# Layer 1 of a conv-attention kernel: the last turns of four blocks by VectorE and DMA, one more half diagonal, and ACT issuing half of the moves

## The chip, the cores and the metric

The kernel runs on one core of a Trainium2 chip. The metric is device time in microseconds (us) of the whole launch. Engines are named as the profile names them: PE (TensorE), DVE (VectorE), ACT (ScalarE), POOL (GpSimd) and SP (SyncE, which here only issues DMAs). ACT issues DMAs too, in order with its own computing.

## What is computed

The reference, cut to what matters (x is 4 images of 128 channels and 4096 positions, float32):

```python
x = x + L0_conv(_gn(x))             # layer 0: attention over the positions, keys of width 64
t = _to_tokens(x)                   # 4 x 4096 tokens of 128
# layer 1, attention: queries and keys are the same matrix q
q = einsum('bsd,de->bse', _ln_t(t), W)
attn = softmax(einsum('bsd,btd->bst', q, q), axis=-1)
t = t + einsum('bst,btd->bsd', attn, _ln_t(t))
# layer 1, recurrence over blocks of the tokens
Wx = einsum('bti,hi->bth', _ln_t(t), W_ffn)    # normalised over the batch
y_t = sigmoid(Wx_t + y_{t-1} @ V.T)            # t = t + y
```

The scores of layer 1 are symmetric: score(s, t) = score(t, s). The kernel uses this.

## The kernel before

**Stages.** One image after the other goes through layer 0 (`layer0`) and layer 1 (`layer1`); after the fourth comes the recurrence (lines 910 to 990). Work on the next image (`prepare`: normalising, queries, keys, values, gates) lies in a list `ahead`, and the closing work of each block in a list `pending`. One entry of one of these is taken per step of the main loops. An empty entry (`nothing`) lets one entry of `ahead` pass. The program is then ordered engine by engine by the tile framework's scheduler, so that an engine's order differs in places from the order of the text[...].

**Layer 1, the pairs.** Tokens form 8 blocks of 512. The loop at line 775 takes n = 6, 7, 5, 4, 3, 2, 1, 0 and, inside, a = n down to 0. A pair (n, a) has two steps (i = 0, 1). In each, PE makes the scores of 512 queries of block n against two tiles of 128 keys of block a (L795, into `ps`, two buffers), ACT turns them into e = exp(score - 48) (L801, four buffers of e), and two steps later (`LAG`) PE adds the direct products h.T @ e to the block's sum `o` (L672, in `direct`). The token matrix h has had 1 added to it, so that the sum over the channels of a result gives the softmax denominator.

For a < n, DVE also turns e in 32x32 blocks into `dd` (L642, two buffers), and 16 DMAs put the blocks into place in `tt` (`send`, L652, three buffers): a quarter f of the rows of `tt` for each of four parts p. Before the change SP issues f = 0, 1, 2 at the end of the pair, and ACT issues f = 3 after the exp of the next step (`unsent`, line 807). Four steps after the pair's end PE multiplies the turned e with the tokens of block n (`reversed_products`, L685), which gives block n's share in block a. `part` (L694, L696) adds up the shares in `oacc`. The tiles `o` and `ot` share three PSUM buffers (`ps_o`).

**The diagonal, a = n.** For n > 1 (`upper`) only the half on and above the diagonal is computed, in columns 512, 384, 256 and 128 wide. Its 6 tiles off the diagonal are turned by DVE (L636), sent (L652, 12 smaller DMAs by SP and 4 by ACT), and multiplied by `own_products` (L662) three steps after the pair, behind that step's direct products. For n < 2 a different way is used: the first step is full, and in the second (`quarter`) PE computes two half-width scores (L581) and makes the rest by four PE transposes of the e before (L587), which ACT copies (L595).

**The end of a block.** When all shares are in, `finish` loads the residual tokens `t` (L722) and queues `tokens`, three empty places, `turn` and `inputs`. `tokens` turns `oacc` by four PE transposes into a PSUM tile (L727, `ps_m`, one buffer), takes the denominators, adds the residual and normalises into h2. `turn` turns h2 by four more PE transposes (L747), ACT copies them into `th` (L748), and the new tokens go out to `t2_d` by `turn_out` (DVE transpose L275, four DMAs L279). `inputs` multiplies `th` with the recurrence's weights (L756). Blocks 7, 6, 5 and 4 are complete in the first half of layer 1, since the pairs that give to them are taken first; blocks 3 to 0 close after pairs of their own.

`move` (used three times per block in layer 0) turns 32x32 blocks by DVE (L275), writes them to DRAM in four DMAs (L279, `turn_d`) and reads them back in place by one (L289): a full turn without PE.

Of the kernel before, what the change touches and what calls it, by code (L numbers as in the profile page):

```python
# [10 lines left out]
F32 = mybir.dt.float32  # L11
# [7 lines left out]
P = 128  # L19
# [153 lines left out]
def fast(  # L173
# [13 lines left out]
    with ExitStack() as st:  # L187
# [124 lines left out]
        def flat(t):  # L312
            return t.rearrange("q p j i -> q (p j i)")
# [237 lines left out]
        def layer1(b, h, qt):  # L551
# [7 lines left out]
            fifo: deque = deque()  # L559
            own_turned: deque = deque()  # L560

            unsent: deque = deque()
            turned: deque = deque()
            clock = 0
# [39 lines left out]

            def upper(n, a):

                return a == n > 1

# [45 lines left out]
            def own_products():  # L656

                _, n, t, o = own_turned.popleft()
                assert fifo and fifo[-1][0] == n
                t = t[:, : 4 * 6 * 32].rearrange("q (p s k) -> q p s k", p=4, s=6)  # L660
                for j, s in ((3, 3), (2, 1), (1, 0)):
                    nc.tensor.matmul(  # L662
                        o[:, : j * P], lhsT=h[:, NQ * n + j, :],
                        rhs=t[:, :, s : s + j, :].rearrange("q p k j -> q k p j"),
                        start=False, stop=False,
                    )
# [25 lines left out]
            def part(n, o):  # L692
# [7 lines left out]
                if parts[n] == NB - n - (b == B - 1 and n == 0):  # L700
                    finish(n)

            def finish(n):
                cs = bass.ts(n, QB)
                rinv = stat.tile([P, NQ], F32, tag="rinv", name="rinv")
                t = work.tile([P, 4, NQ, 32], F32, tag="t", name="t1", bufs=2)
                if b == B - 1 and n == 0:

                    one, two = (ep.tile([P, 2, QB], F32, tag="e", name="last") for _ in range(2))
                    h2, t1 = (one[:, r, :].rearrange("q (j c) -> q j c", j=NQ) for r in range(2))  # L710
                    th = two[:, 0, :]

                    def bank():
                        return ps_s.tile([P, 2, QB], F32, tag="s", name="ml")[:, 0, :]
                else:
                    h2 = work.tile([P, NQ, C], F32, tag="h2", name="h2")
                    th = work.tile([P, QB], F32, tag="th", name="th")
                    t1 = work.tile([P, NQ, C], F32, tag="og", name="t1b")

                    def bank():  # L720
                        return ps_m.tile([P, QB], F32, tag="m", name="m1")
                nc.sync.dma_start(t, t_d[b, n])  # L722

                def tokens():
                    m = bank().rearrange("q (j c) -> q j c", j=NQ)
                    for j in range(NQ):
                        nc.tensor.transpose(m[:, j, :], oacc[:, n, bass.ts(j, P)], ident)  # L727
                    at = (B + b) * NT + n * NQ
                    den = den_all[:, at : at + NQ]
                    nc.vector.tensor_reduce(den, m, AX.X, ALU.add)  # L730
                    nc.vector.tensor_scalar(den, den, 1.0 / C, None, ALU.mult)
                    nc.vector.reciprocal(rinv, den)
                    for j in range(NQ):
                        nc.vector.scalar_tensor_tensor(
                            t1[:, j, :].rearrange("q (p i) -> q p i", p=4),
                            m[:, j, :].rearrange("q (p i) -> q p i", p=4), rinv[:, j : j + 1],
                            t[:, :, j, :], ALU.mult, ALU.add,
                        )
                    layernorm(quarters(t1), quarters(h2))

                def result():
                    turn_out(t1.rearrange("q j (p i) -> q j p i", p=4), t2_d[b, :, cs])

                def turn():
                    m = bank()
                    for j in range(NQ):
                        nc.tensor.transpose(m[:, bass.ts(j, P)], h2[:, j, :], ident)  # L747
                    nc.scalar.copy(  # L748
                        th.rearrange("c (p j k) -> c j p k", j=NQ, p=4),
                        m.rearrange("c (j p k) -> c j p k", j=NQ, p=4),  # L750
                    )
                    result()

                def inputs():
                    m = bank()
                    nc.tensor.matmul(m, lhsT=wt["f"], rhs=th, start=True, stop=True)  # L756
                    nc.vector.bn_stats(bn_st[:, b * NB + n, :], m)
                    m = m.rearrange("p (g i s) -> p i g s", i=L // 2, s=2)
                    if b == B - 1:
                        nc.vector.tensor_copy(wxs[:, :, b, bass.ts(n, GB), :], m)  # L760
                    else:
                        wx = work.tile([P, L // 2, GB, 2], F32, tag="wx", name="wx")
                        nc.vector.tensor_copy(wx, m)
                        nc.sync.dma_start(wxs_d[b, :, :, bass.ts(n, GB), :], wx)

                if b == B - 1 and n == 0:
                    pending.appendleft(tokens)
                    pending.extend([turn, inputs])
                elif b == B - 1 and n < 4:
                    pending.extend([tokens, turn, inputs])  # L770
                else:
                    pending.extend([tokens, nothing, nothing, nothing, turn, inputs])


            for n in [NB - 2, NB - 1] + list(range(NB - 3, -1, -1)):
# [4 lines left out]
                for a in order(n):  # L780
# [4 lines left out]
                    for i in range(2):  # L785
                        ps = ps_s.tile([P, 2, QB], F32, tag="s", name="ps")
                        e = ep.tile([P, 2, QB], F32, tag="e", name="e")
                        if a == n < 2 and i == 1:
                            quarter(n, ps, e, before)
                        else:  # L790
                            width = 0
                            for half in range(2):
                                at = NQ * a + 2 * i + half
                                cols, scores = columns(n, a, i, half, ps)
                                nc.tensor.matmul(  # L795
                                    scores, lhsT=qt[:, bass.ts(at, P)],
                                    rhs=qt[:, n * QB + cols.start : n * QB + cols.stop],
                                    start=True, stop=True,
                                )
                                width += cols.stop - cols.start  # L800
                            nc.scalar.activation(  # L801
                                e.rearrange("p a b -> p (a b)")[:, :width],
                                ps.rearrange("p a b -> p (a b)")[:, :width], AF.Exp, bias=shift,
                            )
                            if turns(n, a) or upper(n, a):
                                turn_tiles(n, a, i, e, packed(d, n, a))
                        if unsent:
                            unsent.popleft()()
                        before = e
                        if o is None:  # L810
                            o = ps_o.tile([P, QB], F32, tag="o", name="o")
                        if n == NB - 2 and i == 0 and a > 0:
                            queries(a - 1)
                        elif n == NB - 2 and a == 0 and i == 1:
                            flush((b, NB - 1))
                            queries(NB - 1)
                        fifo.append((n, a, i, e, o))
                        clock += 1
                        if len(fifo) > LAG:
                            direct()  # L820
                            if a == order(n)[0] and i == 0:
                                direct()
                        if own_turned and own_turned[0][0] <= clock:
                            own_products()
                        if turned and turned[0][0] <= clock:
                            reversed_products()
                        if pending:
                            pending.popleft()()
                        elif ahead:
                            ahead.popleft()()  # L830
                    if turns(n, a) or upper(n, a):
                        send(n, a, d, t, nc.sync, range(3))
                        unsent.append(partial(send, n, a, d, t, nc.scalar, (3,)))
                    if upper(n, a):
                        own_turned.append((clock + 3, n, t, o))
                    elif turns(n, a):
# [555 lines left out]
```

## Time and profile before

| | us |
|---|---|
| runs | 3024.1, 3025.35, 3025.53 (median 3025.35) |
| profiled execution, device time | 3023.71 |
| its span | 3021.6 |
| layer 0, each image (stages 12 to 384, 776 to 1106, 1499 to 1829, 2221 to 2550) | 372, 330, 330, 329 |
| layer 1, each image (384 to 776, 1106 to 1499, 1829 to 2221, 2550 to 2930) | 392, 393, 392, 380 |
| recurrence and end | 91.6 |

How to read the profile's lines: a group line gives line, engine and operation, output<-input, shapes, the count, then busy time and the mean duration in ns, then the engine's idle time just before, with what ended it. A wait line reads "engine, output, line <- what it waited for: total us, times, longest". In lines in order of time the first number is the start from the span's begin, the second the length of the piece. PEld is PE's loading of weights, which runs beside the products. A name ending in q (SPq, ACTq) is the engine's DMA issue. The clock granted to PE was 0.992 of full speed.

### The profile page before, as it was taken

To read this page: it belongs to the slowest core of one execution; us is meant where nothing else is said; L and a number is where in the kernel's file an instruction comes from. 1 tells how busy PE (TensorE), PEld (TensorE's weight loads), DVE (VectorE), ACT (ScalarE), POOL (GpSimd) and SP (SyncE) were. 2 spreads that over 40 slices of the span, in tenths; PEclk is the share of its full clock that TensorE was granted. 3 is DMA by queue.
4 is the path that set the end of the run, shared out by engine and by line. 5 is a ranking of instruction groups with operands and counts; after the bars stand their busy time and mean duration, and the time that the engine had idled before them with its cause. 6 is when DMAs were issued, how large, how long until landed. Compare 5 with 4: busy or idle time off the path is not lost.

```text
span 3021.6 us, 32547 instructions
## 1 busy us (share of the span) xinstructions
PE 2963.2 (98%) x10768; PEld 1381.4 (46%) x10768; DVE 1718.1 (57%) x3210; ACT 1017.0 (34%) x1127; POOL 217.5 (7%) x215
## 2 busy tenths in 40 slices
PE   9999999999999999999999999999999999999985
PEld 4444444444444444444444444444444444444442
DVE  6666654544666664544466666454456666244446
ACT  3444422222344432232244443222234444222224
POOL 0011100000011100000011101000001101000000
PEclk9999999999999999999999999999999999999998
DMA  1111144334112124444311114443411113444433
GB/s 42 41 55 56 46 135 105 97 98 110 28 56 57 50 90 107 106 99 106 72 46 56 51 44 130 104 103 95 106 42 56 50 42 111 129 109 107 103 124 150
DMA packets 265425, 250.62 MB, mean 83 GB/s; under 512 B 96160, under 2 KB 180640, under 8 KB 264224
## 3 DMA queue, kind: packets, MB, share of 16 engines
q1 hardware_dynamic: 239328, 216.95, 26.6%
q10 hardware_dynamic: 25920, 31.49, 4.1%
q8 instruction: 89, 1.46, 0.2%
q14 instruction: 88, 0.72, 0.1%
HBM read 65.80 MB, written 56.62 MB: 41 GB/s over the span
## 4 chain that ended last, share of the span: by engine, by line
PE 94%; DVE 2%; DMA 2%; ACT 1%; SPq 1%; issue 0%; POOL 0%; DVEq 0%; ACTq 0%; POOLq 0%
PE o L476 29%; PE o L672 15%; PE ps L238 15%; PE ps L795 14%; PE ot L685 13%; PE o L662 1%; PE m L756 1%; PE m L267 1%; PE mp L369 1%; PE mp L438 1%; DMA tt<-dd 1%; DMA wxs<-wxs_d 1%; PE mp L423 1%; DVE t2s L976 1%; DVE ps_r L949 1%; SPq L652 1%
## 5 line engine op out<-in xcount | busy, mean ns | idle before, releaser
L476 PE MATMUL o<-e,nxt 64*128 64x512 f32 x4096 | 966.5, 589 | 0.0
L240 ACT ACTIVATE e<-ps 128x1024 f32<-128x1024 f32 x512 | 520.9, 1023 | 688.3 <-PE ps L238 648.8
L247 DVE TENSOR_TENSOR acc<-acc,e 128x1024 f32<-128x1024 f32 x448 | 548.5, 1224 | 229.3 <-ACT e L240 212.7
L476 PEld LDWEIGHTS o<-e,nxt 64*128 64x128 f32 x4096 | 400.5, 187 | 482.6 <-issue 473.8
L801 ACT ACTIVATE e<-ps,shift 128x1024 f32<-128x1024 f32 (+2 forms) x282 | 298.4, 1059 | 730.4 <-PE ps L795 417.0
L238 PE MATMUL ps<-nxt 64*128 64x512 f32 x2048 | 533.3, 595 | 1.2 <-ACT e L240 0.6
L672 PE MATMUL o<-e,h 128*128 128x512 f32 (+3 forms) x1160 | 511.0, 567 | 0.0
L795 PE MATMUL ps<-qt 128*128 128x512 f32 (+3 forms) x1128 | 502.0, 567 | 4.0 <-ACT qt L574 2.7
L642 DVE STREAM_TRANSPOSE dd<-e 128x512 f32<-128x512 f32 x444 | 287.4, 687 | 309.7 <-ACT e L801 215.8
L685 PE MATMUL ot<-tt,h 128*128 128x512 f32 x888 | 402.3, 593 | 0.0
L672 PEld LDWEIGHTS o<-e,h 128*128 128x128 f32 x1160 | 220.3, 191 | 258.5 <-issue 247.9
L795 PEld LDWEIGHTS ps<-qt 128*128 128x128 f32 x1128 | 208.3, 190 | 229.8 <-issue 207.9
L238 PEld LDWEIGHTS ps<-nxt 64*128 64x128 f32 x2048 | 195.1, 187 | 229.4 <-issue 148.8
L685 PEld LDWEIGHTS ot<-tt,h 128*128 128x128 f32 x888 | 164.4, 190 | 186.7 <-issue 185.6
L145 POOL TENSOR_SCALAR rstd<-mv 128x4 f32<-128x4 f32 x64 | 14.5, 226 | 2355.9 <-DVE mv L300 2355.9
L694 DVE TENSOR_TENSOR oacc<-oacc,ot 128x512 f32<-128x512 f32 x87 | 59.4, 682 | 161.8 <-PE ot L685 161.8
L532 DVE SCALAR_TENSOR_TENSOR t<-yt,rinv,t 128x128 f32<-128x128 f32 x128 | 36.5, 347 | 82.4 <-DMA yt<-turn_d 82.4
L543 POOL TENSOR_SCALAR h<-h 128x512 f32<-128x512 f32 x32 | 72.4, 2261 | 63.8 <-DVE d L275 61.7
L493 POOL TENSOR_SCALAR xb<-xb,bpc 128x512 f32<-128x512 f32 x32 | 58.1, 1815 | 245.5 <-DMA xb<-in_x_dram 230.2
L146 POOL TENSOR_TENSOR rstd<-rstd,mhalf 128x4 f32<-128x4 f32 x64 | 66.4, 1037 | 5.3
L381 ACT ACTIVATE nxt<-mp,par 64x512 f32<-64x512 f32 x31 | 23.9, 772 | 115.7 <-DVE nxt L377 99.8
L303 DVE TENSOR_SCALAR h<-t,mv,rstd 128x128 f32<-128x128 f32 x128 | 35.7, 343 | 46.8 <-POOL rstd L146 46.8
(159 smaller groups left out, 1583.8 us busy)
## 6 DMA issues: line engine op xcount, KB each, us to landing
tt<-dd SPq DMA_DIRECT2D x1332, 64.0 KB, 2.0
tt<-dd ACTq DMA_DIRECT2D x444, 64.0 KB, 2.0
turn_d<-d SPq DMA_DIRECT2D x384, 64.0 KB, 1.8
nxt<-in_x_dram SPq DMA_DIRECT2D x16, 512.0 KB, 5.5
xb<-in_x_dram SPq DMA_DIRECT2D x32, 256.0 KB, 3.3
t<-turn_d SPq DMA_DIRECT2D x32, 256.0 KB, 2.7
yt<-turn_d SPq DMA_DIRECT2D x32, 256.0 KB, 2.6
t_d<-t SPq DMA_DIRECT2D x32, 256.0 KB, 2.0
```

Source lines behind the costliest of these rows:

```text
L146: nc.gpsimd.tensor_tensor(dst, dst, mhalf[:, :n], ALU.pow)
L238: nc.tensor.matmul(ps[:, h, :], lhsT=lhsT, rhs=rhs, start=True, stop=True)
L240: nc.scalar.activation(e, ps, AF.Exp, scale=scale)
L247: nc.vector.tensor_tensor(acc, acc, e, ALU.add)
L476: nc.tensor.matmul(o[r], lhsT=v[rs, p + h * PAIRS, :], rhs=e[rs, h, :], start=(p == 0 and h == 0), stop=(p == PAIRS - 1 and h == 1),)
L543: nc.gpsimd.tensor_scalar(hn, hn, 1.0, None, ALU.add)
L642: nc.vector.transpose(d.rearrange("q f b k j -> q k b f j")[:, 2 * i + half], e[:, half, :].rearrange("q (b f j) -> q b f j", b=NQ, f=NQ),)
L672: nc.tensor.matmul(o[:, cols], lhsT=h[:, NQ * a + 2 * i + half, :], rhs=es, start=(a == order(n)[0] and i == 0 and half == 0), stop=(a == ...
L685: nc.tensor.matmul(ot, lhsT=h[:, NQ * n + j, :], rhs=t.rearrange("q (p b k j) -> q b k p j", p=4, b=NQ, k=NQ)[:, j], start=(j == 0), stop= ...
L694: nc.vector.tensor_tensor(oacc[:, n, :], oacc[:, n, :], o, ALU.add)
L795: nc.tensor.matmul(scores, lhsT=qt[:, bass.ts(at, P)], rhs=qt[:, n * QB + cols.start : n * QB + cols.stop], start=True, stop=True,)
L801: nc.scalar.activation(e.rearrange("p a b -> p (a b)")[:, :width], ps.rearrange("p a b -> p (a b)")[:, :width], AF.Exp, bias=shift,)
```

## The change

1. `upper` holds for n > 0: block 1's diagonal is computed as a half as well, and `quarter` remains for n = 0 alone.
2. `own_products` is taken ahead of the step's direct products. (Its check that the newest entry belongs to block n becomes one that some entry does.)
3. Of a turned pair's moves, SP issues f = 0, 1 and ACT f = 2 and f = 3, one each after the exps of the next two steps. A diagonal's moves stay 12 and 4.
4. For n >= 4 `finish` calls `finish_moved`. It turns `oacc` by `move` into `otk` in place of the PE transposes, and after three empty places takes denominators, residual and normalisation from `otk`, with the sum written over `t`; h2 goes by a second `move` into `th` in place of the PE transposes and ACT's copy, the new tokens go out as before, and after three more empty places `inputs` follows (its PSUM tile is `mw`).
5. `reciprocals` and `recurrence_inputs` are these steps of `finish` as functions; their instructions are the same.

```diff
@@ -604,7 +605,7 @@
             def upper(n, a):
-                return a == n > 1
+                return a == n > 0
@@ -656,7 +657,7 @@
             def own_products():
                 _, n, t, o = own_turned.popleft()
-                assert fifo and fifo[-1][0] == n
+                assert any(f[0] == n for f in fifo)
                 t = t[:, : 4 * 6 * 32].rearrange("q (p s k) -> q p s k", p=4, s=6)
                 for j, s in ((3, 3), (2, 1), (1, 0)):
                     nc.tensor.matmul(
@@ -700,7 +701,60 @@
                 if parts[n] == NB - n - (b == B - 1 and n == 0):
                     finish(n)
+            def finish_moved(n):
+
+                cs = bass.ts(n, QB)
+                rinv = stat.tile([P, NQ], F32, tag="rinv", name="rinv")
+                t = work.tile([P, 4, NQ, 32], F32, tag="t", name="t1", bufs=2)
+                nc.sync.dma_start(t, t_d[b, n])
+                ot = th = None
+
+                def sums():
+                    nonlocal ot
+                    ot = work.tile([P, 4, NQ, 32], F32, tag="og", name="otk")
+                    move(oacc[:, n, :].rearrange("c (j f k) -> c j f k", j=NQ, f=4), flat(ot))
+
+                def tokens():
+                    nonlocal th
+                    reciprocals(n, ot.rearrange("q p j i -> q j p i"), AX.XY, rinv)
+                    for j in range(NQ):
+                        nc.vector.scalar_tensor_tensor(
+                            t[:, :, j, :], ot[:, :, j, :], rinv[:, j : j + 1], t[:, :, j, :],
+                            ALU.mult, ALU.add,
+                        )
+                    h2 = work.tile([P, 4, NQ, 32], F32, tag="h2", name="h2m")
+                    layernorm(tiles(t), tiles(h2))
+                    th = work.tile([P, QB], F32, tag="th", name="thm")
+                    move(h2.rearrange("q p j i -> q j p i"), th)
+                    turn_out(t.rearrange("q p j i -> q j p i"), t2_d[b, :, cs])
+
+                def inputs():
+                    recurrence_inputs(n, th, ps_m.tile([P, QB], F32, tag="m", name="mw"))
+
+                gap = [nothing] * 3
+                pending.extend([sums, *gap, tokens, *gap, inputs])
+
+            def reciprocals(n, o, axes, rinv):
+                at = (B + b) * NT + n * NQ
+                den = den_all[:, at : at + NQ]
+                nc.vector.tensor_reduce(den, o, axes, ALU.add)
+                nc.vector.tensor_scalar(den, den, 1.0 / C, None, ALU.mult)
+                nc.vector.reciprocal(rinv, den)
+
+            def recurrence_inputs(n, th, m):
+                nc.tensor.matmul(m, lhsT=wt["f"], rhs=th, start=True, stop=True)
+                nc.vector.bn_stats(bn_st[:, b * NB + n, :], m)
+                m = m.rearrange("p (g i s) -> p i g s", i=L // 2, s=2)
+                if b == B - 1:
+                    nc.vector.tensor_copy(wxs[:, :, b, bass.ts(n, GB), :], m)
+                else:
+                    wx = work.tile([P, L // 2, GB, 2], F32, tag="wx", name="wx")
+                    nc.vector.tensor_copy(wx, m)
+                    nc.sync.dma_start(wxs_d[b, :, :, bass.ts(n, GB), :], wx)
+
             def finish(n):
+                if n >= 4:
+                    return finish_moved(n)
                 cs = bass.ts(n, QB)
                 rinv = stat.tile([P, NQ], F32, tag="rinv", name="rinv")
                 t = work.tile([P, 4, NQ, 32], F32, tag="t", name="t1", bufs=2)
@@ -725,11 +779,7 @@
                     m = bank().rearrange("q (j c) -> q j c", j=NQ)
                     for j in range(NQ):
                         nc.tensor.transpose(m[:, j, :], oacc[:, n, bass.ts(j, P)], ident)
-                    at = (B + b) * NT + n * NQ
-                    den = den_all[:, at : at + NQ]
-                    nc.vector.tensor_reduce(den, m, AX.X, ALU.add)
-                    nc.vector.tensor_scalar(den, den, 1.0 / C, None, ALU.mult)
-                    nc.vector.reciprocal(rinv, den)
+                    reciprocals(n, m, AX.X, rinv)
                     for j in range(NQ):
                         nc.vector.scalar_tensor_tensor(
                             t1[:, j, :].rearrange("q (p i) -> q p i", p=4),
@@ -752,16 +802,7 @@
                     result()
                 def inputs():
-                    m = bank()
-                    nc.tensor.matmul(m, lhsT=wt["f"], rhs=th, start=True, stop=True)
-                    nc.vector.bn_stats(bn_st[:, b * NB + n, :], m)
-                    m = m.rearrange("p (g i s) -> p i g s", i=L // 2, s=2)
-                    if b == B - 1:
-                        nc.vector.tensor_copy(wxs[:, :, b, bass.ts(n, GB), :], m)
-                    else:
-                        wx = work.tile([P, L // 2, GB, 2], F32, tag="wx", name="wx")
-                        nc.vector.tensor_copy(wx, m)
-                        nc.sync.dma_start(wxs_d[b, :, :, bass.ts(n, GB), :], wx)
+                    recurrence_inputs(n, th, bank())
                 if b == B - 1 and n == 0:
                     pending.appendleft(tokens)
@@ -785,7 +826,7 @@
                     for i in range(2):
                         ps = ps_s.tile([P, 2, QB], F32, tag="s", name="ps")
                         e = ep.tile([P, 2, QB], F32, tag="e", name="e")
-                        if a == n < 2 and i == 1:
+                        if a == n == 0 and i == 1:
                             quarter(n, ps, e, before)
                         else:
                             width = 0
@@ -816,12 +857,12 @@
                             queries(NB - 1)
                         fifo.append((n, a, i, e, o))
                         clock += 1
+                        if own_turned and own_turned[0][0] <= clock:
+                            own_products()
                         if len(fifo) > LAG:
                             direct()
                             if a == order(n)[0] and i == 0:
                                 direct()
-                        if own_turned and own_turned[0][0] <= clock:
-                            own_products()
                         if turned and turned[0][0] <= clock:
                             reversed_products()
                         if pending:
@@ -829,8 +870,10 @@
                         elif ahead:
                             ahead.popleft()()
                     if turns(n, a) or upper(n, a):
-                        send(n, a, d, t, nc.sync, range(3))
-                        unsent.append(partial(send, n, a, d, t, nc.scalar, (3,)))
+                        own = 3 if upper(n, a) else 2
+                        send(n, a, d, t, nc.sync, range(own))
+                        for f in range(own, NQ):
+                            unsent.append(partial(send, n, a, d, t, nc.scalar, (f,)))
                     if upper(n, a):
                         own_turned.append((clock + 3, n, t, o))
                     elif turns(n, a):
```

## The prediction

> **What bounds the kernel now.** I read the page's busy times first, then the busy times of the stages, then TensorE's groups by shape, then its order of time, then the waits and the DMA issues.
>
> ```profile
> PE 2963.2 (98%) x10768; PEld 1381.4 (46%) x10768; DVE 1718.1 (57%) x3210; ACT 1017.0 (34%) x1127; POOL 217.5 (7%) x215
> ```
> ```profile
> 384.00:776.00 392.00, 390.70 (x1100) 186.34 (x1098) 195.36 (x419) 110.04 (x122) 12.42 (x19) 1.00 0.41 104
> 2550.00:2930.00 380.00, 366.76 (x957) 172.33 (x956) 155.48 (x370) 89.31 (x95) 12.87 (x19) 0.98 0.43 112
> ```
>
> The second fence is layer 1 of the first and of the last image (after the stage's length: PE, PEld, DVE, ACT, POOL busy). TensorE is idle for 1.3 of 392 us in the first. So inside layer 1 every matmul that goes is time gained, and every wait that appears on TensorE is time lost; nothing else counts until it becomes such a wait.
>
> ```profile
> L662 PE MATMUL o<-tt,h 128*128 128x384 f32 x48 | 20.4, 509 | 5.1 <-DMA tt<-dd 3.6 <-issue 1.5
> L747 PE MATMUL m<-ident,h 128*128 128x128 f32 x124 | 19.5, 276 | 1.1 <-DVE h L303 1.1
> L727 PE MATMUL m<-ident,oacc 128*128 128x128 f32 x124 | 19.5, 279 | 0.0
> L587 PE MATMUL ps<-ident,e 128*128 128x128 f32 x32 | 4.8, 273 | 0.0
> ```
>
> Each float32 product stands as two records, a transpose as one. The one place with a DMA wait of weight is L662, the diagonal block's turned product. A group's busy time overlaps with its neighbours', so I price by the distance from one start to the next:
>
> ```profile
> 496.33 0.66 PE L727 MATMUL m<-ident,oacc 128*128 128x128 f32 x4
> 496.83 1.02 PE L795 MATMUL ps<-qt 128*128 128x512 f32 x2
> ...
> 517.58 0.60 PE L747 MATMUL m<-ident,h 128*128 128x128 f32 x4
> 518.01 1.88 PE L795 MATMUL ps<-qt 128*128 128x512 f32 x4
> ```
>
> Four transposes take 0.50 and 0.43 us. The other blocks read alike (0.44 for L727 at 548.53, 613.61 and 667.43; 0.43 to 0.44 for L747). A record of 512 columns takes 0.43 us (eight in 3.43 us in the chain), so a full product 0.86 us.
>
> [...]the record here has 273 ns, but back to back they cost 0.11 us. [...]
>
> ```profile
> L652 SPq DMA_DIRECT2D tt<-dd x1620: 507/589/5068, 391.3 to 2887.0; - x180
> L652 ACTq DMA_DIRECT2D tt<-dd x540: 514/601/1388, 390.5 to 2880.4; - x180
> ```
>
> **Turns of the upper four blocks.** For blocks 7, 6, 5, 4 of four images both groups of four transposes go: 16 x (0.445 + 0.44) = 14.2 us of TensorE. The copy at L748 (0.58 us, ScalarE) goes too. VectorE gets two more transposes per block (0.71 us, row d<-h): 23 us in all on an engine with 195 of 392 us busy. SP gets ten more issues per block (two moves of four out and one in). These blocks all end in the first half of layer 1, where TensorE has other products queued. A move takes 0.7 (transpose) + 4 x 0.5 (issue) + 1.8 (out) + 0.5 + 2.8 (in) = 7.8 us plus SP's queue, say up to 7 us. The step after three empty places is four steps on; a step has 2 score products, 2 direct ones and half of 4 turned ones, 6 x 0.86 = 5.2 us, so 20 us. In the built order VectorE takes the token step earlier, some two steps (10 us) after the transpose: it may wait a few us for `otk`; behind that stand the part sums and the transposes of e, which have one to two steps to spare (four e buffers, three in ps_o). The last product (`mw`) stands at least four steps after `h2m` is turned. I take 0 here. Without that cover each of the 32 moves would cost TensorE up to some 8 us.
>
> **Diagonal of block 1.** Before: 2 full scores, 2 half scores, 4 transposes, 4 full direct products: 1.72 + 0.86 + 0.44 + 3.43 = 6.45 us. After: scores of 512, 384, 256, 128 columns, 1.50 + 0.65; direct ones the same, 1.50 + 0.65; three turned products, 1.30 (all by distances at the other diagonals): 5.60. Gain 0.85 x 4 = 3.4 us. Its 16 small DMAs have about 15 us of products ahead of their use, as the diagonal of block 2 has; there L662 starts at 721.15 and SP's last issue ends by 716.4, so about 2.7 us remained after landing, with four more issues per pair ahead of it than the change leaves.
>
> **Half of the moves by ACT.** 111 turned pairs: SP 12 to 8 issues, ACT 4 to 8. SP gains 2.4 us per pair. ACT's pair becomes 2 x 1.11 (exp) + 8 x 0.60 = 7.0 us, of 12 x 0.86 = 10.3 us of TensorE. The ACT issues also wait for earlier DMAs of either queue, since the built program hands out eight completion semaphores in turn; behind them on ACT stand the next exp and the copy of the queries, and TensorE's scores wait for those.
>
> ```profile
> ACT e L801 <- PE ps L795: 417.0, 202, 5.8
> ACT e L801 <- DMA tt<-dd: 244.5, 53, 9.7
> ```
>
> In 53 cases an exp came late behind such issues, by 4.6 us on average, of which 2.4 are the four issues themselves; yet TensorE waited for e 1.3 us in total. An exp may be late by most of two steps (two score buffers), some 7 us. So doubling the sends costs between 0 and, if one case in ten goes 3 us over in some 40 places, 12 us. I take 1.5. Below zero I exclude it: TensorE has no idle time in the pairs to win back.
>
> **The turned product before the direct ones.** At a batch's first diagonal nothing hides it:
>
> ```profile
> 400.63 1.88 PE L672 MATMUL o<-e,h 128*128 128x512 f32 x4
> 402.76 1.54 PE L662 MATMUL o<-tt,h 128*128 128x384 f32 x6 [0.24 <-DMA tt<-dd]
> 404.13 1.88 PE L795 MATMUL ps<-qt 128*128 128x512 f32 x4
> ```
>
> The waits are 0.24, 1.52, 0.26 and 3.10 us in the four images: the DMA decides there. Its sends (12 by SP, 4 by ACT) are unchanged and first in SP's queue. In the built order of the change L662's product comes after one more score product in place of two direct ones, so TensorE is there 0.86 us earlier, and in the last image (12 products in place of 16 ahead of it) 3.44 us earlier. The transfer lands when it did, so the waits grow by 3 x 0.86 + 3.44 = 6.0 us; bounds 0 (the landing moves with it) and 4 x 1.72 + 3.44 = 10. At the later diagonals it comes 1.72 us earlier, against 2.7 to 6 us of spare time and shorter queues on SP: 0.
>
> **Sum.** -14.2 - 3.4 + 1.5 + 6.0 = -10.1 us. The profiled execution took 3023.71 us (span 3021.6 and 2.1 around it), 1.6 below the median of 3025.35, so: profiled 3013.6, median 3015.3.
>
> **Rivals.**
> (A) The forecast, 3015.3, with its own range 3010 to 3019.3.
> (B) The first diagonals' waits don't grow and ACT costs nothing: 3025.35 - 17.6 = 3007.8. For it: SP's queue is shorter everywhere. Against: at the first diagonal it is the same queue.
> (C) Late exps, or diagonals that wait at blocks 5, 4 and 3, where a move's five issues (2.8 us) now stand in SP's queue by the diagonal's twelve: 16 places x 0.5 us or so on top, 3019.3 to 3031.4, likeliest 3023. For it: spare times of 3 to 6 us less 1.72 less 2.8 come near zero. Against: SP has four issues fewer per pair ahead of it.
> (D) Slower: ACT becomes the bound in turned pairs. Its 7.0 us leave 3.3 us for waiting in two groups of sends, so from 1.65 us per group on, every pair is ACT's. The late exps show 4.6 - 2.4 = 2.2 us, but in 53 cases of 135 groups. If all groups waited 1.8 us: 0.3 x 111 = 33 us, so 3015.3 + 33 = 3048. Against: shorter SP queues shorten just these waits.
> That the change doesn't do what it says is ruled out: the built order has 64 transposes fewer at each of the two lines, and ACT 1000 sends in place of 540.
>
> **Chances.** A 0.53, B 0.20, C 0.19, D 0.08. This kernel's measurement tells about 0.2% (6 us) from no change: faster is below 3019.3: A and B, 0.73; same 0.19; slower 0.08. The range takes in B's time with a little below it and most of C: 3006 to 3024.
>
> **What would show it.** TensorE busy about 18 us less; L727's and L747's rows at half their count; the idle time ahead of the 384-column turned product near 11 us, all at the batches' starts; exps put down to `tt<-dd` in about twice as many cases, and TensorE's wait for e still below 5 us; no wait of TensorE for `thm`. Wrong would be: idle time of tens of us at the score products behind ACT, at `mw`, or at the diagonals of blocks 5 to 1.

## The result, and the profile after

The changed kernel takes 3016.79 us, the median of nine runs, against 3024.48 us, the median of nine runs of the kernel before beside it (3023.0 to 3025.85). That is 7.7 us less, a ratio of 0.9976 [0.9967, 0.9984]: faster by slightly more than the 0.2% that the prediction took as the least that can be told. One of the nine runs took 3565.5 us at a granted clock of 0.846 and is left out of the ratio; the other eight lie between 3015.10 and 3019.59 us, with a median of 3016.43.

The profiled execution took 3016.79 us with a span of 3015.1 us: 6.9 and 6.5 us less than the one before, where the sum of the prediction had 10.1. In the fences that follow come first the busy times of the page, then the same two stages of layer 1 that were shown of the kernel before:

```profile
PE 2945.1 (98%) x10648; PEld 1368.4 (45%) x10648; DVE 1744.4 (58%) x3258; ACT 1005.0 (33%) x1107; POOL 220.7 (7%) x215
```
```profile
384.00:776.00 392.00, 390.13 (x1084) 184.97 (x1083) 203.57 (x432) 108.23 (x118) 12.42 (x19) 1.00 0.46 116
2550.00:2930.00 380.00, 357.12 (x906) 167.21 (x905) 163.51 (x382) 82.88 (x85) 13.78 (x22) 0.97 0.46 121
```

TensorE is busy 18.1 us less (2963.2 to 2945.1), and the span is only 6.5 us shorter: so its idle time grew by 11.6 us. In the first image it is still idle for only 1.9 of 392 us. In the last one it is idle for 22.9 of 380. TensorE's groups by shape say where the new idle time stands:

```profile
L663 PE MATMUL o<-tt,h 128*128 128x384 f32 x56 | 23.7, 505 | 12.1 <-DMA tt<-dd 11.2 <-issue 0.9
L797 PE MATMUL m<-ident,h 128*128 128x128 f32 x60 | 10.1, 282 | 2.8 <-DVE h L303 2.8
L781 PE MATMUL m<-ident,oacc 128*128 128x128 f32 x60 | 9.4, 279 | 1.0 <-DVE wx L752 1.0
L745 PE MATMUL mw<-thm,w 128*128 128x512 f32 x32 | 16.3, 592 | 0.0
```

The transposes of the sums and of `h` stand at 60 in place of 124 (four more of each, for the last block, are listed under `ml`, before and after), and TensorE is idle for nothing ahead of the product `mw`, whose input comes by a turn through DRAM. The diagonal's turned product lost 7.0 us more than before (12.1 against 5.1). The other 4.6 us are small: 1.7 at L797, 1.0 at L781, 0.9 at the score products, 1.1 in the final recurrence.

The 7.0 us stand in one place: the last image's first diagonal waits 7.3 us longer, the other three together 0.3 us less. Here is TensorE in order of time at the first diagonal of the last image:

```profile
2562.87 1.12 PE L574 MATMUL mq<-qt,w 128*128 128x512 f32 x2 [0.68 <-ACT qt L575]
2574.43 2.90 PE L663 MATMUL o<-tt,h 128*128 128x384 f32 x6 [10.43 <-DMA tt<-dd]
```

It waits 10.43 us there, where it waited 3.10. In the other three images the same product waits 0, 0.94 and 0.76 us, where it waited 0.24, 1.52 and 0.26. SyncE's order of time ahead of it, of the change and then of the kernel before:

```profile
2541.03 10.00 SPq L939 DMA_DIRECT2D wxs<-wxs_d  x3
2558.76 14.27 SPq L653 DMA_DIRECT2D tt<-dd  x12
```
```profile
2552.47 10.06 SPq L896 DMA_DIRECT2D wxs<-wxs_d  x3
2563.09 17.03 SPq L652 DMA_DIRECT2D tt<-dd  x12
```

The three large loads of the last image stand ahead of the diagonal's sends in both. From the issue of the first load to the first send of the diagonal 10.6 us pass before, 17.7 after, and to the product that needs the last of them 29.2 and 33.4 us. So the transfer itself came 4.2 us later, counted from the loads; the rest of the longer wait is that TensorE is there sooner.

The trace shows what holds the transfer. In it each DMA of SyncE and ScalarE (2922 before, 3146 in the change) carries one of eight completion semaphores, which tell of its landing and go round over both queues. Of the 2914 and 3138 DMAs that follow another one on their semaphore, none starts before that one has landed; in 1034 and 1084 cases that one is of the other engine's queue. In the change only one of SyncE's twelve sends goes out ahead of the third load's landing. The second has that load's semaphore, stands 6.8 us, starts 0.02 us after the load has landed, and the other ten follow it. Before, five had gone out, and seven followed after a wait of 4.4 us. SyncE's waits of this stretch, the change's and then the one before:

```profile
SPq L653 <- DMA wxs<-wxs_d: 6.8, 1, 6.8
```
```profile
SPq L652 <- DMA wxs<-wxs_d: 4.4, 1, 4.4
```

Four more of ScalarE's sends have taken four places of the rotation. So four more sends, 0.63 us apart, follow the load, and the load itself lands 1.8 us later (25.1 in place of 23.3 us after the first one's issue): together about the 4.2 us.

Last, ScalarE's and SyncE's waits at the sends, the change's own:

```profile
ACT e L842 <- DMA tt<-dd: 371.6, 74, 15.8
```
```profile
SPq L653 <- DVE dd L643: 201.7, 72, 6.7
```

Exps come late behind the sends in 74 cases in place of 53 (371.6 us in place of 244.5), where the prediction expected about twice as many cases. SyncE stands 201.7 us waiting for VectorE's data ahead of its sends (116.2 before): I take that as its reserve.

### The profile page after: what moved, and what is told of

The parts are those of the page before. It is cut to its first block, busy times and chain, and to the rows that moved or that the text cites. A ratio compares the mean times of both kernels' runs of the same rounds, so it can differ in the third digit from the quotient of the medians.

```text
span 3015.1 us, 32597 instructions
## 1 busy us (share of the span) xinstructions
PE 2945.1 (98%) x10648; PEld 1368.4 (45%) x10648; DVE 1744.4 (58%) x3258; ACT 1005.0 (33%) x1107; POOL 220.7 (7%) x215
## 4 chain that ended last, share of the span: by engine, by line
PE 94%; DVE 3%; DMA 1%; ACT 1%; SPq 0%; issue 0%; POOL 0%; ACTq 0%; DVEq 0%; POOLq 0%
PE o L476 29%; PE o L673 15%; PE ps L238 15%; PE ps L836 14%; PE ot L686 13%; PE o L663 1%; PE m L267 1%; PE mp L369 1%; DMA wxs<-wxs_d 1%; PE mp L438 1%; PE mp L423 1%; DVE t2s L1019 1%; DVE ps_r L992 1%; PE mq L574 1%; PE m L745 0%; PE ps_r L1005 0%
## 5 line engine op out<-in xcount | busy, mean ns | idle before, releaser
L145 POOL TENSOR_SCALAR rstd<-mv 128x4 f32<-128x4 f32 x64 | 14.5, 226 | 2342.0 <-DVE mv L300 2342.0
L637 DVE STREAM_TRANSPOSE dd<-e 128x128 f32<-128x128 f32 (+1 forms) x112 | 35.3, 353 | 54.2 <-ACT e L842 45.8
```

## The experiments

Each was timed beside the kernel before. "Above the change" below compares differences to the kernel before; the change's is -7.7 us. The 95% intervals reach 2 to 5 us to either side, so that differences of 1 or 2 us between two runs are not told apart. Two theories stood at the start: that the parts cost what the prediction's sum says, with the extra loss at the first diagonals; and that the gain is lost elsewhere, to ScalarE's doubled sends.

**Each part undone by itself.** First, block 1's diagonal again in halves:

```diff
-                return a == n > 0
+                return a == n > 1
-                        if a == n == 0 and i == 1:
+                        if a == n < 2 and i == 1:
```

> The change with block 1's diagonal computed as before (full first step, quarter for the second). If the half diagonal is worth what its products cost, TensorE is busy 3.4 us longer than in the change and the time is about 3020 us, 3.4 above the change's 3016.8. If the wait for its sends, or the other order at the end of the layer, eats this, the time stays at 3016.8.

3021.22 us, ratio 0.9989 [0.9982, 0.9996]: 4.4 us above the change, where 3.4 was priced. In the profile TensorE is busy 7.1 us longer (2952.2) and idle 2.1 us less, not busy 3.4 us longer as expected; what the rest of the 7.1 us is stays open.

Second, the turned product behind the direct ones again, block 1 apart:

```diff
-                        if own_turned and own_turned[0][0] <= clock:
+                        if own_turned and own_turned[0][0] <= clock and own_turned[0][1] == 1:
                             own_products()
                         if len(fifo) > LAG:
                             direct()
                             if a == order(n)[0] and i == 0:
                                 direct()
+                        if own_turned and own_turned[0][0] <= clock:
+                            own_products()
```

> The change with the turned product of the diagonal behind the step's direct products again, except for block 1, whose sum would be closed by then. If its place sets the wait at the first diagonal of an image, the wait in the last image falls from 10.4 to about 7.0 us (TensorE gets there 3.4 us later, the transfer lands when it did) and the others from 1.7 to about 0, so some 5 us less in all: 3012. If the transfer's landing moves with TensorE, or the waits come from elsewhere, it stays at 3016.8.

3012.18 us, ratio 0.9958 [0.9944, 0.9972]: 4.7 us below the change, so this part cost 4.7 us, where 6.0 was taken. Only one half of the expectation came: the waits of the other three images did not fall (1.77 us in all, 1.70 in the change). TensorE in order of time, at the last image's first diagonal:

```profile
2566.16 1.12 PE L574 MATMUL mq<-qt,w 128*128 128x512 f32 x2 [0.68 <-ACT qt L575]
2574.37 2.90 PE L663 MATMUL o<-tt,h 128*128 128x384 f32 x6 [7.09 <-DMA tt<-dd]
```

The product starts at the same time as in the change (2574.37 and 2574.43); what lies ahead of it ends 3.3 us later. The wait is the transfer's, and the earlier place only uncovers more of it.

Third, SyncE sends three quarters again:

```diff
-                        own = 3 if upper(n, a) else 2
+                        own = 3
```

> The change with SP issuing three quarters of a turned pair's moves again and ACT one. If ACT's second group of sends holds SP's first diagonal sends back in the last image (the eight completion semaphores go round over both queues), SP begins them some 10 us after the loads instead of 17.7, and the wait there is about 6.5 us instead of 10.4: 3013, and late exps behind sends fall from 74 to about 55 cases. If SP needs the relief (22 issues per pair and move), waits appear at later diagonals or turned products and the time is 3020 or more.

3063.12 us, ratio 1.0130 [1.0115, 1.0146]. That is 46 us above the change. What the expectation says of the last image's first diagonal came: SyncE begins it 10.9 us after the loads' issue, and TensorE waits 6.95 us there in place of 10.43. But what it says of SyncE's relief came too, and far outweighs that gain: I had held the relief for worth nothing. SyncE's waits and TensorE's group in this run:

```profile
SPq L653 <- DMA tt<-dd: 134.4, 90, 4.0
SPq L653 <- DVE dd L643: 13.3, 7, 3.6
```
```profile
L663 PE MATMUL o<-tt,h 128*128 128x384 f32 x56 | 27.0, 567 | 33.8 <-DMA tt<-dd 33.0 <-issue 0.8
```

SyncE's reserve is gone (13.3 us in place of 201.7): the data now waits for SyncE, and TensorE for the data, 33.8 us at the diagonals in place of 12.1. In layer 1 of the first image (390 to 782 us) SyncE's 512 issues add up to 299 us, and it waits 40 us more until earlier sends have landed; in the change (390 to 776) its 401 issues add up to 236 us. The waits are no longer at the images' first diagonals only:

```profile
686.85 1.79 PE L663 MATMUL o<-tt,h 128*128 128x384 f32 x6 [2.17 <-DMA tt<-dd]
728.07 2.06 PE L663 MATMUL o<-tt,h 128*128 128x384 f32 x6 [2.21 <-DMA tt<-dd]
```

The idle time explains 24.6 us. The other 18.8 us stand as busy time: 2963.9 us for the same 10648 records. Part of it is the clock. TensorE at the first of these waits, in three stretches (us, busy time, records, granted clock, DMA share, GB/s):

```profile
684.00:688.00 4.00, 1.83 (x6) 1.00 0.23 57
688.00:691.40 3.40, 3.40 (x7) 0.50 0.43 105
691.40:704.00 12.60, 12.60 (x31) 1.00 0.56 149
```

After 2.17 us of waiting the clock is halved for 3.4 us, which costs another 1.7 us. Over the 20 us from 684 us the granted clock is 0.91, and as low over the 20 us from 724 us, around the wait of 2.21 us. A longer wait of the same run did nothing of the kind, with a granted clock of 1.00 over the 20 us from 1416 us:

```profile
1416.64 1.54 PE L663 MATMUL o<-tt,h 128*128 128x384 f32 x6 [2.87 <-DMA tt<-dd]
```

Half speed came in multiples of one length: in the change's own trace its three stretches start at 2566.13, 2917.70 and 2992.80 us, 103 and 22 times 3.413 us apart, and the first two last 13.65 us, four times 3.413 (the third runs to the end). What makes a wait of 2.17 us halve the clock and one of 2.87 us not was not shown.

Over the span the granted clock is 0.988 against 0.992, worth 36.7 less 24.1 = 12.6 us (with the rounding, 9.5 to 15.6) at most, since half-speed time can fall on an idle TensorE (in the change 8.3 of the 13.65 us from 2566.13 do). The rest of the 18.8 us stays open. So does the part of the built order: the scheduler gave TensorE another one here, with 16 direct products in a row behind the diagonal of the first wait, where the change alternates them with scores (first this run, then the change behind its own diagonal):

```profile
688.44 8.50 PE L673 MATMUL o<-e,h 128*128 128x512 f32 x16
```
```profile
679.14 1.88 PE L673 MATMUL o<-e,h 128*128 128x512 f32 x4
680.86 1.88 PE L836 MATMUL ps<-qt 128*128 128x512 f32 x4
```

Fourth, no moves at all:

```diff
-                if n >= 4:
-                    return finish_moved(n)
```

> The change without the new closing of blocks 7 to 4: both turns of them by TensorE again. If the moves are hidden, TensorE is busy 14.2 us longer and the idle time stays near 70 us: 3031 us, slower than before. If the moves cost waits, part of the 4.6 us of idle time that is new elsewhere than at the diagonals goes with them and the time is 3026 to 3030.

3029.99 us, ratio 1.0019 [1.0012, 1.0026]: 13.1 us above the change, where 14.2 was priced. TensorE is busy 14.5 us more (2959.6), its idle time nearly the same (68.3 and 70.0 us). So the moves are worth what their 128 transposes took, and hidden.

**Why does SyncE's share decide?** Two crossings of the third edit:

```diff
-                        own = 3 if upper(n, a) else 2
+                        own = 3
... with the second edit, or with the fourth
```

> As e3 (SP issues three quarters), with the diagonal's turned product behind the direct ones again (except block 1). If e3's waits come from the product being 1.7 us too early for a slower SP queue, most of its 46 us over the change go: 3015 to 3025. If SP's queue itself is too long (12 issues per turned pair and 10 more per moved block) the later place buys 1.7 us of 2 to 4 us at each late diagonal: 3045 to 3058.

> SP issues three quarters and blocks 7 to 4 are turned by TensorE again, so of the change only the half diagonal of block 1 and the earlier product remain. If e3 is slow because the moves' issues fill SP, this is near the kernel before: 3024.5 - 3.4 + 6 = 3027. If e3 is slow because of the half diagonal or the earlier product with SP's long queue, it is 3050 or more.

With the product back behind the direct ones: 3058.66 us, ratio 1.0114 [1.0098, 1.0129]; its place is not the cause (the diagonals wait 21.1 us in place of 33.8, and 3.9 us are won). Without the moves: 3026.83 us, ratio 1.0008 [1.0000, 1.0017]. So with SyncE at three quarters the moves cost 36 us (38.6 less 2.8 above the kernel before), and at half they win 13. The two parts only work together.

The pair of runs without moves also prices ScalarE's doubled sends alone: +5.4 us to the kernel before with them, +2.8 without, so 2.6 us, where 1.5 was taken. The two intervals overlap, so that the times alone don't show it. It is seen at one place, the last image's first diagonal, with half of the sends by ScalarE and then with a quarter, both without moves:

```profile
2586.26 2.90 PE L663 MATMUL o<-tt,h 128*128 128x384 f32 x6 [9.89 <-DMA tt<-dd]
```
```profile
2583.30 2.90 PE L663 MATMUL o<-tt,h 128*128 128x384 f32 x6 [6.11 <-DMA tt<-dd]
```

That is 3.8 us more there. At the other diagonals together the run with half of the sends waits 1.6 us less, which leaves 2.2 us.

**Are the large loads what delays that diagonal?** The second edit again, and the three loads of 2 MB later, in `ahead`, kept in program order:

```diff
-                for i in range(B - 1):
-                    nc.sync.dma_start(wxs[:, :, i, :, :], wxs_d[i])
+                ahead.extend([lambda: None] * 12)
+                for i in range(B - 1):
+                    ahead.append(partial(load_wx, i))
+                    ahead.extend([lambda: None] * 3)
```

> As e2, and the three loads of the recurrence's inputs (2 MB each), which SP issues ahead of the last image's first diagonal, spread over later steps of that layer. If the loads make the 7 us wait left in e2, it goes and the time is about 3005. If the wait is due to the sends alone, as in the other images, no more than 1 us is gained; if the loads now delay later transfers, 7 us are lost again elsewhere: 3012.

3009.76 us, ratio 0.9952 [0.9938, 0.9965]. The first diagonal's wait is gone (7.09 us with the second edit alone, none here), so the loads made it. The time fell by only 1.9 us against the second edit alone, inside the intervals. In the wait's place a turned product waits 5.14 us behind one of the moved loads, for whose landing SyncE stood 12.4 us:

```profile
2663.43 6.49 PE L686 MATMUL ot<-tt,h 128*128 128x512 f32 x8 [5.14 <-DMA tt<-dd]
```

**Are the three empty places the moves' cover?**

```diff
-                gap = [nothing] * 3
+                gap = []
```

> The change without the empty places between the steps of the moved closing. The built order of VectorE has the token step at the same place as before the edit, two steps behind the transpose, and only the last product comes some four steps earlier. If the scheduler's order hides the move and not the empty places, the time stays at 3016.8 within 2 us. If they are the cover, TensorE waits for the moved h2 at the last product, up to 8 us in each of 16 blocks: 3025 to 3100.

3018.94 us, ratio 0.9983 [0.9976, 0.9990]: 2.6 us above the change, with overlapping intervals. TensorE now waits at `mw`, but little:

```profile
PE mw L745 <- DMA thm<-turn_d: 1.2, 4, 0.4
```

The built order leaves VectorE's token step where it was, so most of the cover is the scheduler's. But the empty places are the reserve. In the first of these blocks `mw` starts 19.2 us after `thm` has landed with them (521.12 to 540.30), and at once without them (521.31 to 521.35).

**A better version?** The loads in twelve pieces of 512 KB, with the second edit:

```diff
+                ahead.extend([lambda: None] * 12)
+                ahead.extend(partial(load_wx, i, j) for i in range(B - 1) for j in range(4))
```

> As e7, with each of the three loads cut in four pieces of 512 KB, one per step. e7 left one wait of 5.1 us at a turned product that stood behind a whole load. If the load's length in front of the sends was its cause, it goes: about 3005 us. If SP has no room for nine more issues there, waits of 2 us or more appear at the diagonals of that layer and it is no faster than e7's 3009.8.

3008.46 us, ratio 0.9949 [0.9936, 0.9963]: the lowest median of all, 14.9 us below the kernel before and 7.2 below the change, but not told apart from the whole loads (3009.76) or from the second edit alone. The 3005 did not come: a later diagonal of the last image now waits 6.22 us. One of the pieces stands right ahead of its sends (issued at 2702.20, landed at 2707.64), and the wait ends at 2711.10. Then moves for more blocks on top, in the first three images:

```diff
-                if n >= 4:
+                if n >= (4 if b == B - 1 else 2):
... and then 1 in place of 2
```

> As e9, with the closing by moves for blocks 3 and 2 too in the first three images: six more blocks, 5.3 us less of TensorE's transposes. If the cover holds at the end of a layer as in its first half, 5 us under e9: about 3000. If SP's queue is the limit there (e3: it falls behind by 2 us and more at just these blocks' diagonals), waits take it back: e9's time or more.

> As e10, with block 1 too (nine more blocks than e9, 8.0 us less of TensorE's transposes). Block 1 closes when the layer ends, so its moves run beside layer 0 of the next image, where SP has room: another 2.6 us under e10. If the next image's first steps wait for its closing, no gain over e10.

3011.35 us, ratio 0.9962 [0.9948, 0.9975], and 3009.7 us, 0.9954 [0.9940, 0.9967]: no gain over the pieces alone that these runs can tell. With blocks 3 and 2, TensorE is busy 5.0 us less (2938.6 against 2943.6), and this wait is new:

```profile
PE mw L745 <- DMA thm<-turn_d: 5.8, 3, 2.8
```

These waits come where the layer ends and the products of the next image's layer 0 have begun:

```profile
768.14 1.12 PE L745 MATMUL mw<-thm,w 128*128 128x512 f32 x2 [1.24 <-DMA thm<-turn_d]
769.20 1.13 PE L238 MATMUL ps<-nxt 64*128 64x512 f32 x4
```

So there is other work, but TensorE's order puts `mw` ahead of it, sooner than the turn has landed. A later place for `mw` was not tried.

## Why the prediction was right, point by point

It forecast 3015.3 us with a range of 3006 to 3024, and faster; 3016.79 came. The median is nearer than the gain: the kernel before took 3024.48 us beside it, not 3025.35, so that 7.7 us were gained where 10.1 were forecast. Undone one by one, the parts give -13.1 - 4.4 + 4.7 + 2.6 = -10.2 us; the 2.5 us that this has too much are no more than these runs leave uncertain. Its bound was the right one: layer 1 is TensorE's, and what TensorE doesn't do is won, less its new waits.

- **"128 transposes, 14.2 us"**: 13.1 when undone. Pricing by the distance of starts (0.44 us for four) was right; by the records' own 276 ns it would have been 35 us.
- **"Diagonal of block 1, 3.4 us"**: 4.4 when undone.
- **"I take 0" for the moves' waits**: held, with TensorE idle for nothing at `mw`. The reason given, four steps between the parts, was only half of it: without the empty places 1.2 us of waiting appear, so the built order hides the moves and the empty places are the reserve. That SyncE had the time for the moves was not priced (last point).
- **"At the later diagonals 0"**: held in the change.
- **Earlier turned product, 6.0 us**: 4.7 when undone. "The transfer lands when it did", and 0.86 us in each of the first three images: not so there. They lost nothing in sum (2.02 us before, 1.70 after). In the last image the product came some 3.1 us earlier, as priced (3.44), and the transfer 4.2 us later, which was not priced. That the idle time at this product came "near 11 us" (12.1) is therefore partly luck: 2.6 us that did not come were made up for by 4.2 us that were not foreseen.
- **ScalarE's sends, 1.5 us**: 2.6 without moves. The late exps, for which it was taken, stayed harmless (74 cases, TensorE waits 1.9 us for e in all). The cost stands where the prediction said that the sends were "unchanged and first in SP's queue": the last image's first diagonal. There twelve of ScalarE's sends, in place of eight, come after the loads' issue began and before SyncE is through with the diagonal's, and eleven of SyncE's twelve are left to wait for the third load's landing, in place of seven. The prediction knew the rotation of the eight completion semaphores, but counted it for the exps alone. The trace shows this wait; no run changes the rotation by itself.
- **All idle time "at the batches' starts"**: 7.0 of the 11.6 us. The 4.6 us at L797, L781, the score products and the recurrence are missing in the sum. No run isolates them. They and the larger price of the sends may be what is missing from the gain.
- **"SP gains 2.4 us per pair"**, given no value: the large omission. It didn't show because the change has it, and in this the prediction was lucky. Without it the moves' ten issues per block and twelve sends per pair overfill SyncE, and the kernel is 46 us slower. A prediction of the moves alone, by the same steps, would have been wrong in sign.

Of the rivals, B (no growth of the waits) fell by 7.0 us of growth, C (late diagonals) by waits of nothing there, D (ScalarE the bound) by TensorE's 1.9 us of waiting for e. But the run with SyncE at three quarters shows C's mechanism at work as soon as SyncE is not relieved.

## What to carry to other kernels

Add up a DMA-issuing engine's issues like any other engine's work: at 0.59 us each, twelve sends take SyncE 7.1 of a pair's 10.3 us, eight take 4.7. Here only the latter left room for ten issues of moves per block besides, since SyncE also waits for earlier transfers to land (with twelve, 40 us in layer 1 of the first image). Its wait for data ahead of its sends shows the reserve (201.7 us with eight, 13.3 with twelve). Work moved off the bounding engine paid nearly its full price here (13.1 of 14.2 us) where that engine had other work between its parts, and gained nothing in the blocks that close at the end of a layer. Look at what stands ahead of a small transfer that is waited for at once. A large load there cost TensorE 7.1 us; taken away, or cut in pieces, it made waits of 5.1 and 6.2 us at later places. And when two engines' DMAs share their completion semaphores, as they do here, count both engines' sends ahead of a small transfer: with twelve of ScalarE's in place of eight, eleven of SyncE's twelve stood until a large load had landed, in place of seven.

## What the runs showed of the hardware

- A wait of TensorE can cost nearly twice its length: 2.17 us idle were followed by 3.4 us at half the clock, 1.7 us more. After waits of 2.87 and 2.64 us in the same run the six records took 1.54 us and the granted clock stayed at 1.00, so it isn't the length alone. What else it is was not shown.
- A send's issue takes 0.59 us of SyncE's time and its transfer 2.1 us to landing, both medians of the change's trace. When one of SyncE's sends starts there, 3.5 of its transfers are under way on average, itself among them, and six at most. With twelve sends per pair and the moves, SyncE's queue, its issues and its waits for earlier landings together, was the limit: moving four of twelve sends per pair to another engine is worth 46 us in this kernel. How much of it is the issue time alone was not isolated.
